# A four-layer graph network on one core: PSUM banks in the schedule, fewer row transposes, weights behind x, the last graph in pieces

## The chip, the core and the metric

The kernel runs on one core of a Trainium2 chip. The core has a matrix engine (TensorE, PE in the profile; PEld is its loading of stationary operands), a vector engine (VectorE, DVE), a scalar engine with activation functions (ScalarE, ACT), a general engine (GpSimd, POOL) and an engine that mainly issues transfers (SyncE, SP). Each works through its own queue in order and waits on semaphores for the others. Matmuls write to PSUM, which has eight banks here, each a tile of 128 x 512 floats; DVE and ACT read the results out. The metric is the time of the whole program on the device in microseconds, of several runs; a profile of one execution stands beside it.

## The reference

There are 32 graphs of 512 nodes with 256 features, x of (32, 512, 256), and adj of (32, 512, 512), integers of 0 and 1. Four layers follow each other, each with its own kind of attention over the graph, on a normalised and rectified input and with a residual:

```python
h = maximum(layernorm(x), 0)
x = x + layer(h, adj, ...)        # four times, layers 0 to 3

# layer 0: att = softmax(((h @ att_W) @ h.T) / 16 + mask); twice: h = tanh(att @ (h @ W + b))
# layer 1: Wh = h @ W.T; e = leaky(src[:, None] + dst[None, :]); softmax over adj > 0; att @ Wh
# layer 2: Hh = h @ W; e = exp(-leaky(s[:, None] + d[None, :])) where adj != 0; elu((e @ Hh) / rowsum)
# layer 3: hW = h @ W; logits = (hW @ a_1).T + hW @ a_2 + (hW @ a_12) @ hW.T
#          att = softmax(leaky(logits) over adj > 0); elu(h @ W_1 + (att @ h) @ W_2)
```

All products are in fp32. The graphs don't depend on each other; within a graph each layer depends on the one before.

## The kernel before

The kernel takes a graph as four tiles of 128 nodes. It doesn't run in a loop at the time of execution: a planner at build time puts all instructions of all 32 graphs in one order, with up to FLIGHT = 5 graphs in progress, so that one graph's matmuls run while another's vector work is done.

Each step of the computation is an `op`: an engine, a cost as a pair (how long it holds its engine, when its result is there), the ops it comes after, a function that emits it, and the tiles it uses. Tiles come from numbered places in pools: 35 pages of SBUF, four value buffers, eight PSUM banks and a few more. `Plan.order` plays the ops through event by event: at each moment every engine takes, of its ready ops, the one with the earliest due time whose places are free. The due time is the graph's number times a distance, less what is still to come after the op; the distance of the last graphs is another one. `Plan.best` tries 32 pairs of distances and keeps the one whose order ends first by the planner's own clock. The ops are then emitted in that order, which fixes the sequence on each engine and each issuing queue; semaphores for the tiles' dependences are added by the framework below, and it, not the plan, decides who waits at run time.

A graph's work runs as follows. x and the adjacency come in by SP's queue (L458, L461); DVE turns the integers into a code, SP's transposing transfers turn it (L478), and masks are made of it. `normed` computes statistics on DVE (L496, L497), a power on POOL (L503), an offset on DVE (L506) and the normalised row on ACT (L510). The result is turned by a transfer on SP (L518) in two 16-bit planes and joined by ACT (L530); the first graph's first layer is turned by PE (L523, out at L526) instead.

Layers 0 and 3 do their block products with seven products in place of eight (`seven`): sums of blocks are formed on DVE (L600), then seven matmuls go alternately into a part p and a part q that accumulate in PSUM, and after each stage a block is copied out by ACT or added to another by DVE before the next product goes into the same place. With `beside` set, p and q are two halves of one bank: bank_f0p and bank_f3p (features, L715, copied out at L723 or L725, added at L730), bank_v0p and bank_w3p (values, L741). Without it, they are two banks: bank_q0p and q0q (L806), bank_s3p and s3q (L983), bank_v3p and v3q (L741).

Layers 1 and 2 need one row of scores spread over all partitions (`leaky_exp_t`). For the first and last five graphs, `turned`, PE makes it by four transposes of a broadcast column (L654, bank_r) and ACT reads it from PSUM (L671). For the others, DVE transposes squares (L658), SP writes the row to DRAM (L662) and reads it back spread over the partitions (L667), and ACT reads it from SBUF.

`attend` (L698, bank_a) multiplies the exponentials with the values for two tiles of nodes at a time, and a column of ones in the values gives the row sums. In layer 0 a second convolution follows (L851, L869). Behind layer 3, `fourth` takes reciprocals (L1063) and adds both terms (L1068), upper3, exp4 and all_terms (L1074, L1078, L1081) make the elu and the residual for two tiles each, and POOL's queue stores the graph in one transfer (L1092).

The weights come in at the start: att_W and W0, which the first graph needs, by ACT's queue (L384), and DVE forms their seven block sums (L361 to L366); the others by POOL's queue (L306), after the first graph's adjacency.

Of the kernel before, what the change touches and what calls it, by code (L numbers as in the profile page):

```python
# [15 lines left out]
AF = mybir.ActivationFunctionType  # L16
# [3 lines left out]
P = 128  # L20
# [8 lines left out]

PE512, PE256, PET = 429.0, 216.0, 112.0
def pe(n512=0, n256=0, nt=0):
    t = n512 * PE512 + n256 * PE256 + nt * PET
    return t, t + 170.0


# [15 lines left out]
class Plan:  # L53
# [3 lines left out]

    PASS = 200.0  # L60


    APART, APART_LAST = [1000.0 * k for k in range(32, 64, 2)], [1000.0 * k for k in (2, 8)]
    LAND, RATE = 2000.0, 200.0
    SLACK = {"V": (1.05, 0.0), "A": (1.05, 0.0), "G": (1.5, 0.0), "D": (1.0, 800.0)}

# [3 lines left out]
    def op(self, engine, cost, after, emit, graph, uses=(), size=0):  # L70


        much, more = self.SLACK.get(engine, (1.0, 0.0))
        cost = cost[0] * much, cost[1] * much + more
        flat = []
        for a in after:
            flat += a if isinstance(a, tuple) else [a]
        o = {"engine": engine, "cost": cost, "after": [a for a in flat if a is not None], "emit": emit,
             "graph": graph, "uses": list(uses), "number": len(self.ops), "size": size, "late": more}
        self.ops.append(o)  # L80
        return o

# [5 lines left out]
    def best(self, pools):  # L88
        for o in self.ops:
            o["depth"] = 0  # L90
        again = True
        while again:
            again = False
            for o in self.ops:
                depth = max((a["depth"] + 1 for a in o["after"]), default=0)
                again |= depth > o["depth"]
                o["depth"] = max(depth, o["depth"])
        apart = min(itertools.product(self.APART, self.APART_LAST), key=lambda a: self.order(pools, *a)[1])
        out, took = self.order(pools, *apart)
        assert len(out) == len(self.ops), "the plan is stuck"  # L100
        return out, took

    def order(self, pools, apart, apart_last):
        free = {pool: list(range(n)) for pool, n in pools.items()}
        users = {}
        for o in self.ops:
            o["left"] = len(o["after"])
            for p in o["uses"]:
                p["users"] = 0
                p.pop("number", None)  # L110
            for a in o["after"]:
                users.setdefault(a["number"], []).append(o)
# [21 lines left out]
        while True:  # L134
            for e in engines:
                skipped = []
                while at[e] <= now and ready[e]:
                    rank, o = heapq.heappop(ready[e])
                    new = [p for p in o["uses"] if "number" not in p]
                    need = [p["pool"] for p in new]  # L140
                    if any(len(free[n]) < need.count(n) for n in need):
                        skipped.append((rank, o))
                        continue
                    for p in new:
                        p["number"] = free[p["pool"]].pop(0)
                    holds, until = o["cost"]
                    if o["size"]:
                        wire = max(wire, now) + o["size"] / self.RATE
                        until = wire - now + self.LAND + o["late"]
                    at[e] = now + holds  # L150
                    out.append(o)
                    heapq.heappush(events, (at[e], next(numbers), None))
                    heapq.heappush(events, (now + until + self.PASS, next(numbers), o))
                for x in skipped:
                    heapq.heappush(ready[e], x)
            if not events:
                break
            now = events[0][0]
            while events and events[0][0] <= now:
                o = heapq.heappop(events)[2]  # L160
                if o is None:
                    continue
                for p in o["uses"]:
                    p["users"] -= 1
                    if not p["users"]:
                        free[p["pool"]].append(p["number"])
                for w in users.get(o["number"], []):
                    w["left"] -= 1
                    if not w["left"]:
                        heapq.heappush(ready[w["engine"]], (w["rank"], w))  # L170
        return out, now if len(out) == len(self.ops) else float("inf")


@with_exitstack
def kernel(
# [35 lines left out]
    HALF = H // 2  # L211
    FLIGHT = 5
    PAGES, VALUES = 35, 4
    LEAD = 2

    const = ctx.enter_context(tc.tile_pool(name="const", bufs=1))
# [81 lines left out]
    def prepare(engine, cost, after, emit, *keys, size=0):  # L298
        return plan.op(engine, cost, after, emit, 0, W.uses(keys), size)
# [80 lines left out]

    ready = {}
    w0_sb, att_sb = raw("raw9"), raw("raw10")
    for n, dst, w, key in (("att", att_s, att_w, "raw10"), ("w0", w0_s, w0, "raw9")):
        ready[key] = [prepare("A", (550.0, 4000.0), [], lambda w=w, key=key: nc.scalar.dma_start(  # L384
            out=raw(key)(), in_=rows_of(w)), key, size=P * HC * H * 4)]
        ready[n] = seven_of(raw(key), dst, HALF, ready[key], key)
    nc.scalar.dma_start(out=b0_sb, in_=line_of(b0))
# [47 lines left out]
    def graph(b, adj_before, x_before):  # L435
# [4 lines left out]
        def op(engine, cost, after, emit, *keys, size=0, weights=()):  # L440
            return plan.op(engine, cost, after, emit, b, T.uses(keys) + W.uses(weights), size)

        def two(g):
            return slice(2 * g, 2 * g + 2)
# [7 lines left out]
        def e(l, c):  # L452

            return T[f"e{l}_{c // 2}"][:, c % 2, :]
# [12 lines left out]
        for t in range(NT):  # L467

            got_adj.append(op("D", D_ADJ, got_adj[-1:] if b else [], partial(fetch_adj, t), "adj", size=P * N * 4))
        if b == 0:  # L470
            for o in loads:
                o["after"] += got_adj[-1:]

# [17 lines left out]
        def normed(l, xs):  # L491
# [41 lines left out]
            done = []  # L533
            for g in range(NT // 2):
                a, d = (op("V", V_STATS, [xs[t]], partial(stats, t), "x", "slot") for t in (2 * g, 2 * g + 1))
                a = op("V", V_TINY, [a, d], partial(variance, g))
                r = op("G", G_POW, [a], partial(root, g))
                r = op("V", V_TINY, [r], partial(offset, g))
# [81 lines left out]
        def scored_values(l, hs, w_aug, ready):  # L620
# [4 lines left out]
            for t in range(NT):  # L625
# [10 lines left out]
                def values(t, key):  # L636
                    nc.scalar.copy(T[f"v{l}"][:, t, LEAD : LEAD + H], T[key][:, :H])  # L637

                a = op("PE", pe(n256=4), [hs[t]] + ready, partial(product, t, key), key, f"hT{l}")
                ss.append(op("V", V_TINY, [a], partial(scores, t, key), key))  # L640
                vs.append(op("A", A_HALF, [a], partial(values, t, key), key, f"v{l}"))
            return vs, ss
# [1 line left out]
        def leaky_exp_t(l, ss, sign):  # L644
# [1 line left out]

            turned = b < FLIGHT or b >= B - FLIGHT
            key = f"bank_r{l}" if turned else f"row{l}"  # L650
            line = []

# [34 lines left out]
        def attend(l, es, vs, use):  # L687


            done, a = [], None  # L690
            lead = LEAD if l < 3 else 0
            for g in range(NT // 2):
                keys = [f"bank_a{l}{2 * g + j}" for j in range(2)]

                def product(g, c, keys):
                    for j in range(2):
                        t = 2 * g + j
                        nc.tensor.matmul(T[keys[j]][:, : LEAD + H + 1 - lead], e(l, c)[:, t * P : (t + 1) * P],  # L698
                                         T[f"v{l}"][:, c, lead:], start=(c == 0), stop=(c == NT - 1))

                for c in range(NT):
                    a = op("PE", pe(n256=4), [es[c], vs[c], a], partial(product, g, c, keys),
                           *keys, f"v{l}", f"e{l}_{c // 2}")
                done += [use(2 * g + j, a, keys[j]) for j in range(2)]
            return done


        def two_tiles(key, start, k):
# [361 lines left out]
            a = op("V", V_TINY, [a], sums, key)  # L1070
            return op("V", V_PSUM, [a, wb[0, t // 2], wb[1, t // 2]], both_terms, key, "y3", "w3")

        def upper3(g):
            nc.vector.scalar_tensor_tensor(T["x"][:, two(g), :], T["y3"][:, two(g), :], -1.0, T["x"][:, two(g), :],  # L1074
                                           ALU.max, ALU.add)

        def exp4(g):
            nc.scalar.activation(T["r3"][:, two(g), :], T["y3"][:, two(g), :], AF.Exp, bias=one)  # L1078

        def all_terms(g):  # L1080
            nc.vector.scalar_tensor_tensor(T["y3"][:, two(g), :], T["r3"][:, two(g), :], 1.0,  # L1081
                                           T["x"][:, two(g), :], ALU.min, ALU.add)

        us = attend(3, es, vs, fourth)
        last = []
        for g in range(NT // 2):
            u = op("V", V_MASK, us[two(g)], partial(upper3, g), "y3", "x")
            l = op("A", A_BIAS, us[two(g)], partial(exp4, g), "y3", "r3")
            last.append(op("V", V_MASK, [l, u], partial(all_terms, g), "y3", "r3", "x"))

        def store():
            nc.gpsimd.dma_start(out=out[b].rearrange("(t p) h -> p t h", p=P), in_=T["y3"])  # L1092

        op("G", G_STORE, last, store, "y3", "slot", "ahead", size=N * H * 4)
        return code, got_x[-1]

    code, got_x = None, [None, None]
# [40 lines left out]
```

## Time and profile before

| | us |
|---|---|
| median of 3 runs | 2413.71 (2413.61 to 2414.37) |
| profiled execution | 2412.91 |
| its span, first to last instruction | 2411.1 |
| PE busy in the span | 2370.4 |
| DVE busy | 2052.5 |
| ACT busy | 1720.6 |
| first matmul begins | 13.46 |
| last run of matmuls begins, and lasts | 2396.03, 7.27 |

The granted clock of PE is 0.999 of full speed. Busy time counts an engine's instructions from start to end; matmuls are pipelined and their ends are modelled, so that they overlap, and the profile's busy PE is not PE at its peak. The time from one matmul's start to the next says more. An instruction of the code that multiplies in fp32 shows in the profile as two matmuls of the same width; a transpose shows as one. Where the profile names a releaser, it is the engine and line whose semaphore came last by the records. Line numbers are those of the kernel before; in the changed kernel the same instructions stand some 32 to 42 lines further down.

### The profile page before, as it was taken

The page shows a single profiled execution, that of the slowest core. Times are in us where ns is not written, and L with a number is a line of the kernel's source. Part 1 is how long each engine was busy: PE and PEld are TensorE (multiplying, and loading weights), DVE is VectorE, ACT ScalarE, POOL GpSimd, SP SyncE. Part 2 cuts the span into 40 slices and gives each one's busy share as a digit, 9 for nine tenths or more (in the row PEclk, how much of TensorE's full clock was granted, in tenths as well). Part 3 has the DMA queues.
Part 4 walks back from the last instruction along what each step waited for, and adds up shares of the span by engine and source line. Part 5 has one row for each costly group of instructions (what it writes and reads, how often), then busy time and mean ns, then how long its engine had stood idle before and what let it go on. Part 6 is the DMA issues. An engine that isn't in the chain of part 4 may idle for free.

```text
span 2411.1 us, 36568 instructions
## 1 busy us (share of the span) xinstructions
PE 2370.4 (98%) x11638; PEld 1983.9 (82%) x11638; DVE 2052.5 (85%) x6316; ACT 1720.6 (71%) x3385; POOL 262.3 (11%) x320
## 2 busy tenths in 40 slices
PE   7999999999999999999999999999999999999998
PEld 5788888888888888888888888888888888887877
DVE  6778889888898888888888988888888898876888
ACT  4567777677777777767777777777777777665885
POOL 3000011101110100101110111101011100110110
PEclk9999999999999999999999999999999999999999
DMA  7311333333323333333323334333333343320221
GB/s 190 90 42 38 73 69 88 74 71 63 86 67 74 86 73 74 82 65 82 84 62 84 72 72 87 70 77 76 67 85 84 62 88 75 84 44 18 49 44 44
DMA packets 429633, 175.55 MB, mean 73 GB/s; under 512 B 385824, under 2 KB 402848, under 8 KB 429440
## 3 DMA queue, kind: packets, MB, share of 16 engines
q1 hardware_dynamic: 423392, 153.81, 30.0%
q0 software_dynamic: 5360, 18.75, 2.5%
q8 instruction: 92, 1.51, 0.3%
q14 instruction: 101, 0.83, 0.1%
q10 hardware_dynamic: 688, 0.66, 0.1%
HBM read 64.49 MB, written 16.87 MB: 34 GB/s over the span
## 4 chain that ended last, share of the span: by engine, by line
PE 90%; issue 3%; ACT 3%; DVE 2%; DMA 2%; SPq 0%; POOL 0%; POOLq 0%; DVEq 0%; ACTq 0%
PE bank_a L698 35%; PE bank_z L851 9%; PE bank_v L630 8%; PE bank_o L869 5%; PE bank_q0p L806 4%; PE bank_s3p L983 4%; PE bank_v0p L741 4%; PE bank_f0p L715 4%; PE bank_w3p L741 4%; PE bank_f3p L715 4%; PE bank_q0q L806 3%; PE bank_s3q L983 3%; PE bank_v3p L741 2%; PE bank_v3q L741 2%; DMA planesT<-planes 1%
## 5 line engine op out<-in xcount | busy, mean ns | idle before, releaser
L698 PE MATMUL bank_a<-v,e 128*128 128x257 f32 (+1 forms) x4096 | 977.3, 381 | 3.2 <-ACT e L1035 1.5
L698 PEld LDWEIGHTS bank_a<-v,e 128*128 128x128 f32 x4096 | 758.0, 190 | 152.4 <-issue 47.9
L503 POOL TENSOR_TENSOR rstd<-ve,mhalf 128x2 f32<-128x2 f32 x256 | 223.0, 884 | 1947.7 <-DVE ve L500 1668.9
L530 ACT COPY hT<-planesT 128x512 uint16<-128x512 uint16 x508 | 380.7, 768 | 70.1 <-DMA planesT<-planes 69.3
L510 ACT ACTIVATE xn<-x,off,rstd 128x256 f32<-128x256 f32 x512 | 277.0, 595 | 45.0 <-DVE off L506 44.6
L630 PE MATMUL bank_v<-l_aug,hT 128*128 128x258 f32 x1024 | 253.6, 381 | 0.5 <-ACT hT L530 0.4
L851 PE MATMUL bank_z<-e,y 128*128 128x512 f32 x512 | 240.7, 592 | 0.7 <-ACT y L842 0.7
L515 DVE COPY planes<-xn 128x512 uint16<-128x512 uint16 x508 | 206.6, 422 | 19.1 <-DMA planesT<-planes 13.7
L630 PEld LDWEIGHTS bank_v<-l_aug,hT 128*128 128x128 f32 x1024 | 190.9, 190 | 28.2 <-ACT hT L530 1.5
L496 DVE BATCH_NORM_STATS2 st<-x 128x6 f32<-128x256 f32 x512 | 210.1, 410 | 0.0
L674 ACT ACTIVATE e<-e 128x512 f32<-128x512 f32 x256 | 151.7, 625 | 0.0
L851 PEld LDWEIGHTS bank_z<-e,y 128*128 128x128 f32 x512 | 95.5, 190 | 68.1 <-issue 56.4
L671 ACT ACTIVATE e<-row,scores 128x512 f32<-128x512 f32 x176 | 118.0, 711 | 13.9 <-DMA row<-row 13.7
L637 ACT COPY v<-bank_v 128x256 f32<-128x256 f32 x256 | 89.2, 376 | 53.8 <-PE bank_v L630 43.9
L869 PE MATMUL bank_o<-w_sb,zT 128*128 128x256 f32 x512 | 120.2, 379 | 0.0
L990 DVE SCALAR_TENSOR_TENSOR e<-bank_s3p,v,mask 128x256 f32<-128x256 f32 x256 | 111.0, 476 | 6.2 <-PE bank_s3p L983 5.1
L497 DVE BATCH_NORM_AGGREGATE mv<-st 128x2 f32<-128x6 f32 x512 | 93.2, 182 | 17.5
L869 PEld LDWEIGHTS bank_o<-w_sb,zT 128*128 128x128 f32 x512 | 96.5, 190 | 13.9 <-DVE st L496 0.2
L725 ACT ACTIVATE fa<-bank_f3p,l_u 128x256 f32<-128x256 f32 x128 | 60.5, 472 | 66.0 <-PE bank_f3p L715 65.6
L814 ACT ACTIVATE e<-e 128x512 f32<-128x512 f32 x93 | 58.6, 630 | 54.6 <-DVE e L823 54.1
L829 DVE TENSOR_TENSOR e<-e,mask 128x512 f32<-128x512 f32 x124 | 85.0, 686 | 9.4 <-ACT e L814 9.3
L892 DVE TENSOR_TENSOR e<-e,mask 128x512 f32<-128x512 f32 x128 | 84.0, 688 | 5.4 <-ACT e L674 5.1
(189 smaller groups left out, 4462.8 us busy)
## 6 DMA issues: line engine op xcount, KB each, us to landing
adj<-in_adj_dram SPq DMA_DIRECT2D x128, 256.0 KB
out_dram<-y POOLq DMA_DIRECT2D x32, 512.0 KB, 4.2
x<-in_x_dram SPq DMA_DIRECT2D x31, 512.0 KB
row<-row SPq DMA_DIRECT2D x44, 256.0 KB
planesT<-planes SPq DMA_TRANSPOSE x508
codeT<-code SPq DMA_TRANSPOSE x128
crest<-crest SPq DMA_TRANSPOSE x64
raw_w<-in_L_gnn_W_dram POOLq DMA_DIRECT2D x3, 256.0 KB, 4.7
```

What stands on the lines that cost most here:

```text
L496: nc.vector.bn_stats(T[f"st{l}"][:, t, :], T["x"][:, t, :])
L503: nc.gpsimd.tensor_tensor(T[f"rstd{l}"][:, two(g)], T[f"ve{l}"][:, two(g)], mhalf[:, two(g)], ALU.pow)
L510: nc.scalar.activation(T[f"xn{l}"][:, t, :], T["x"][:, t, :], AF.Relu, bias=T[f"off{l}"][:, t : t + 1], scale=T[f"rstd{l}"][:, t : t + 1])
L515: nc.vector.tensor_copy(T[f"planes{l}_{t}"], bits)
L530: nc.scalar.copy(bits[:, :, :, t * P : (t + 1) * P], T[f"planesT{l}_{t}"].rearrange("p (b c) n -> p b c n", b=2))
L630: nc.tensor.matmul(T[key][:, :cols], T[f"hT{l}"][:, c, t * P : (t + 1) * P], w_aug[:, c, :], start=(c == 0), stop=(c == HC - 1))
L698: nc.tensor.matmul(T[keys[j]][:, : LEAD + H + 1 - lead], e(l, c)[:, t * P : (t + 1) * P], T[f"v{l}"][:, c, lead:], start=(c == 0), stop=(c ...
L715: nc.tensor.matmul(p[:, : N // 2], w[:, x - 1, :], right(x), start=fresh, stop=True, skip_group_check=True)
L741: nc.tensor.matmul(p[:, j * k : (j + 1) * k], right(x)[:, j * P : (j + 1) * P], w[:, x - 1, :], start=fresh and j == 0, stop=True, skip_gr ...
L806: nc.tensor.matmul(p[:, j * N // 2 : (j + 1) * N // 2], right(x)[:, j * P : (j + 1) * P], left(x), start=fresh and j == 0, stop=True, skip ...
L851: nc.tensor.matmul(T[f"bank_z{k}"], T["y0"][:, c, k * P : (k + 1) * P], e(0, c), start=(c == 0), stop=(c == NT - 1))
L869: nc.tensor.matmul(T[key][:, j * H : (j + 1) * H], T["zT"][:, k, t * P : (t + 1) * P], w1_sb[:, k, :], start=(k == 0), stop=(k == HC - 1))
```

## The change

Four things change. In the planner, `order` no longer lets an op use a PSUM bank while another engine's op in that bank has not ended by the plan's clock, and the pairs of distances are compared by `replay`, which runs a finished order once more with plain costs (without the planner's allowances), with 100 ns for every hand-over between ops, and with the rule that users of a place wait for the former owner and, in a bank, for other engines' users. A price for a matmul of 258 columns is new. Second, PE makes the rows by transposes for the first and last two graphs (TURNED) in place of five. Third, W0 and att_W are issued by SP, behind x of the first graph, their block sums come behind the statistics of the first graph, and the first graph's adjacency comes behind both weights. Fourth, the last graph's last attention is done for tiles 0 and 1 together, then for tile 2, then for tile 3, with the elu by the same parts and a store of each by SP's queue.

```diff
-        apart = min(itertools.product(self.APART, self.APART_LAST), key=lambda a: self.order(pools, *a)[1])
-        out, took = self.order(pools, *apart)
+        apart = min(itertools.product(self.APART, self.APART_LAST), key=lambda a: self.replay(self.order(pools, *a)))
+        out = self.order(pools, *apart)
+        took = self.replay(out)
...
+    def replay(self, order):
...
+        at, end, owners, before, wire = {}, {}, {}, {}, 0.0
+        for o in order:
+            start = max([at.get(o["engine"], 0.0)] + [end[a["number"]] + self.HOP for a in o["after"]])
+            for p in o["uses"]:
+                where = p["pool"], p["number"]
+                owner = owners.get(where)
+                if owner is None or owner[0] is not p:
+                    before[where] = owner[1] if owner else []
+                    owner = owners[where] = p, []
+                waits = before[where]
+                if p["pool"] == "bank":
+                    waits = waits + [x for x in owner[1] if x["engine"] != o["engine"]]
+                start = max([start] + [end[x["number"]] + self.HOP for x in waits])
+                owner[1].append(o)
+            holds, until = o["plain"]
+            if o["size"]:
+                wire = max(wire, start) + o["size"] / self.RATE
+                until = wire - start + self.LAND
+            at[o["engine"]], end[o["number"]] = start + holds, start + until
+        return max(end.values())
...
-                    if any(len(free[n]) < need.count(n) for n in need):
+                    if any(len(free[n]) < need.count(n) for n in need) or any(
+                            t > now for p in o["uses"] if p["pool"] == "bank" for x, t in p["ends"].items() if x != e):
...
+                    for p in o["uses"]:
+                        p["ends"][e] = now + until + self.PASS
...
+    TURNED = 2
...
-    for n, dst, w, key in (("att", att_s, att_w, "raw10"), ("w0", w0_s, w0, "raw9")):
-        ready[key] = [prepare("A", (550.0, 4000.0), [], lambda w=w, key=key: nc.scalar.dma_start(
+    for n, dst, w, key in (("w0", w0_s, w0, "raw9"), ("att", att_s, att_w, "raw10")):
+        ready[key] = [prepare("D", D_X, [], lambda w=w, key=key: nc.sync.dma_start(
...
+            for n in ("raw9", "raw10"):
+                ready[n][0]["after"] += got_x[-1:]
+            for o in got_adj[1:]:
+                o["after"] += ready["raw9"] + ready["raw10"]
...
+                if b == l == 0:
+                    for n in ("w0", "att"):
+                        ready[n][0]["after"].append(d)
...
-            turned = b < FLIGHT or b >= B - FLIGHT
+            turned = b < TURNED or b >= B - TURNED
...
+            return [[0, 1], [2], [3]] if (b, l) == (B - 1, 3) else [[0, 1], [2, 3]]
...
+        def store_part(ts):
+            nc.sync.dma_start(out=out[b].rearrange("(t p) h -> p t h", p=P)[:, ts, :], in_=T["y3"][:, ts, :])
...
+            if b == B - 1:
+                op("D", D_OUT, last[-1:], partial(store_part, ts), "y3", "slot", "ahead", size=N * H)
...
-        op("G", G_STORE, last, store, "y3", "slot", "ahead", size=N * H * 4)
+        if b < B - 1:
+            op("G", G_STORE, last, store, "y3", "slot", "ahead", size=N * H * 4)
```

## The prediction

> **What bounds the kernel now.** I read the page's engine shares first, then the chain of waits, then the groups of TensorE (PE) by shape, the list of waits, and last the timeline at the start, at one stall in the middle and at the end.
>
> The page's engine shares, and the shares of its chain of waits by engine: PE is busy throughout, and the chain is PE nearly throughout.
>
> ```profile
> PE 2370.4 (98%) x11638; PEld 1983.9 (82%) x11638; DVE 2052.5 (85%) x6316; ACT 1720.6 (71%) x3385; POOL 262.3 (11%) x320
> ...
> PE 90%; issue 3%; ACT 3%; DVE 2%; DMA 2%; SPq 0%; POOL 0%; POOLq 0%; DVEq 0%; ACTq 0%
> ```
>
> Two of PE's groups by shape (count, busy us and mean ns, idle before), two of its waits (us, times, longest), and two runs of the chain in order of time (start, length, count): the mean of one matmul is well over what one takes in a run, and the waits of PE that recur are for readers of bank_f0p.
>
> ```profile
> L698 PE MATMUL bank_a<-v,e 128*128 128x257 f32 x3072 | 729.5, 380 | 1.6 <-ACT r L935 0.8 <-DVE e L919 0.6 <-DVE e L892 0.2
> L654 PE MATMUL bank_r<-ident,scores 128*128 128x128 f32 x80 | 21.7, 273 | 0.0
> PE bank_f0p L715 <- ACT fa L723: 8.2, 20, 0.5
> PE bank_f0p L715 <- DVE fa L730: 1.7, 4, 0.4
> 528.39 2.62 PE bank_v L630 x12
> 558.20 13.01 PE bank_a L698 x60
> ```
>
> The timeline (start, length) at the start, at one such stall, and at the end: what the first matmul comes behind, who is in the bank between two matmuls, and what follows the last one.
>
> ```profile
> 6.81 0.29 DVE L361 COPY att_s<-raw_w 128x256 f32<-128x256 f32 x1 [5.93 <-DMA raw_w<-in_L_gnn_att_W_dram]
> 8.09 0.42 DVE L496 BATCH_NORM_STATS2 st<-x 128x6 f32<-128x256 f32 x1
> 13.46 0.97 PE L523 MATMUL bank_n<-ident,xn 128*128 128x128 f32 x3 [13.46 <-ACT xn L510]
> 531.70 0.59 PE L715 MATMUL bank_f0p<-hs,att_s 128*128 128x256 f32 x2
> 532.13 0.61 PE L741 MATMUL bank_v3p<-l_aug,hT 128*128 128x129 f32 x4
> 532.33 0.42 DVE L730 TENSOR_TENSOR fa<-fa,bank_f0p 128x256 f32<-128x256 f32 x1 [0.66 <-PE bank_f0p L715]
> 532.79 0.37 ACT L723 COPY fa<-bank_f0p 128x256 f32<-128x256 f32 x1 [0.85 <-DVE fa L730]
> 533.21 0.70 PE L715 MATMUL bank_f0p<-hs,att_s 128*128 128x256 f32 x2 [0.47 <-ACT fa L723]
> 2396.03 7.27 PE L698 MATMUL bank_a<-v,e 128*128 128x259 f32 x32 [0.17 <-ACT e L1035]
> 2405.11 0.69 DVE L1081 SCALAR_TENSOR_TENSOR y<-r,x 128x512 f32<-128x512 f32 x1
> 2406.10 0.75 POOL L1092 DMA_DIRECT2D out_dram<-y  x1 [4.88 <-DVE y L1081]
> ```
>
> So PE is the bound. Its busy time overlaps itself (a mean of 380 ns, yet 60 in a row in 13.01 us), so I count by pitch, the time from one start to the next in an unbroken run. 257 columns: 13.01/60 = 0.217 us. 258: 2.62/12 = 0.218. 256: 16 in 3.45 = 0.216. 512: 0.429. 128 or 129: 0.111. With the counts by shape: 3072 x 0.217 + 2047 x 0.218 + 3190 x 0.216 + 536 x 0.429 + 2760 x 0.111, and 3 for the narrow ones, is about 2341 us. The span is 2411.1. Of the other 70 us, 13.5 lie before the first matmul, 7.8 behind the last (2403.30 to 2411.1), and about 49 are holes. Those three are all that a reordering can win; only removed matmuls lower the 2341.
>
> **What the Trainium skill says.** "PSUM — Partial Sum Buffer", section on bank collisions, says that two engines must not be in the same bank and quadrant at once, two readers included, and that software must guard by bank. The trace agrees with the consequence: at 532.33 VectorE (DVE) reads bank_f0p, ScalarE (ACT) reads other columns of it only afterwards (532.79, released by DVE), and PE writes it again only after that (533.21). "DMA: Bandwidth & Descriptors", section "Latency and other measured facts", gives about 0.6 us to the first byte for a transfer issued by SP and about 1 us by POOL, and under "Issuing engines are not separate DMA queues" that all issuers share the same 16 DMA engines. For the first, no SP store of output exists in this trace; the second agrees with the start, where x and two weights, issued by two engines within 2 us, all come late.
>
> **The change part by part.**
>
> Row transposes. TURNED 2 in place of FLIGHT 5 takes graphs 2, 3, 4 and 27, 28, 29 off the PE route: 6 graphs x 2 layers x 4 = 48 of the 80 transposes of L654. At a pitch of 0.111 us that is 5.3 us of PE work, and PE is the bound: -5.3. In their place come 12 square transposes on DVE (0.305 each, 3.7 us over the run, beside PE), 24 SP transfers (0.55 and 0.53 to issue), and 48 ACT passes at 711 ns in place of 692. In the middle 44 such trips show no wait of PE for a row, only 13.7 us of ACT in 14 waits. I take 0 for this cost; from above see the last rival.
>
> Bank rule in the plan (order, replay). No instruction changes; the order does. A block in seven goes PE, then one or two readers of its bank, then PE into the same bank. That trip is 0.6 us with one reader (0.16 us of matmul tail, a read of 0.37, two hand-overs) and 533.21 - 532.13 = 1.08 with two. PE needs that much other work in between. From the two orders of instructions I summed PE's own work at its pitch between one matmul of a bank and the next one into it that carries a wait. Before, 94 such places have under 0.9 us of cover (37 in f0p, 21 f3p, 14 v0p, 17 w3p, 5 elsewhere); after, 23. Missing cover against a trip of 0.9 is 19.7 us before and 4.0 after; against 0.7, 10.6 and 2.3; against 1.1, 38.8 and 8.7. The middle fits the trace: PE's waits for readers of these banks add up to 13.7 us in about 36 waits, and 0.16 of tail in each makes 19.5. So -16, with -8 and -30 as ends.
>
> What the new order may add. Pulling blocks apart delays their consumers and uses cover that other waits had: exponentials for L698, normalised rows for L630. The order alone can't show those. Below: 0, since PE has always one of five graphs to work on. Above: 10 us, a third of the roughly 30 us of holes not caused by these banks. I take +3.
>
> Weights behind x. At present the DVE stands at L361 until 6.81 for att_W, and only then comes the first statistic of x; L361 to L366 for W0 (9.17 to 10.4) stand between its second and third. After: W0 and att_W are issued on SP behind x of graphs 0 and 1, both L361 blocks behind all statistics and the first offset. x alone then has the DMA engines after b0: 0.64 MB, which the start moved by about 5 us (bins of 1 us: 0, 37, 102, 146, 251, 366 GB/s, slow at first). Four statistics of 0.6 from about 4.8 end at 7.2, 0.2 for variance, 1.0 for POOL, 0.2 for the offset, 0.65 for ACT: first matmul at 9.3, not 13.46. Then the adjacency, now behind x of graphs 2 and 3 and both weights, is later: 3.7 MB ahead of its end in place of about 2.8, some 14 to 15 us, not 11.92. Four turns (12.73 to 18.02 to issue, mask at 23.03) lead from there to the mask at about 26, and the first L698, now at 31.6, may start at about 27 with the products before it done. SP queues x and adjacency of later graphs behind it, needed much later. Gain -4.2; ends -1 (the mask decides) and -5.5.
>
> Last graph in pieces. The first pair of tiles leaves earlier, the third and fourth tile one by one; PE's 32 matmuls stay 32. After PE's last, today: reciprocal, two L1068 (0.85), exponential 0.72, L1081 0.69, to 2405.80; with one tile 0.43, 0.47 and 0.42, so 0.85 less. The store: packets of 512 KB ran some 1.6 us at 350 GB/s, 128 KB needs 0.4; minus 1.2, and SP rather than POOL perhaps 0.3 more against a further queue entry. -2.2, ends -1 and -3.5. PE258 in place of PE256 only changes the plan's price.
>
> Sum against the profiled execution: -5.3 - 16 + 3 - 4.2 - 2.2 = -24.7, span 2386.4. That execution took 2412.91, 1.8 above its span, and the median is 2413.71, 0.8 above it: 2389.
>
> **Rivals.** (1) The waits move. The banks' holes close, but PE meets others, for exponentials and normalised rows, and the mask takes most of the start's gain: -5.3 - 8 + 5 - 1.5 - 1.5, about -12, 2402. For it: ACT waits already 44.6 us for offsets and 69.3 for turned planes. Against: PE hardly waits for these now.
> (2) More falls than the banks' part: with trips priced at 1.1 and no new waits, -5.3 - 28 - 4 - 2.2 is -39, 2374. For it: 49 us of holes. Against: drain and fill keep some.
> (3) Nothing to measure: replay's order differs but the machine's queues absorb it, and the mask eats the start: -5.3 + 3, 2411.
> (4) Slower: the row's trip is exposed. In the middle it takes from the first L662 at 395.7 to the first L671 at 404.1, 8.4 us, hidden by four other graphs. Graphs 2 to 4 and 27 to 29 run where fewer are in flight and SP is busiest. 12 x 8.4 is 101 us; it outweighs the 25 gained from a quarter exposed. At half: 2389 + 50, about 2439. For it: the second slice from the start and the one at 2280 to 2340 (56.33 us busy of 60) hold larger holes already. Against: no PE wait for a row in 44 trips.
>
> **How the numbers follow.** Forecast 0.60, its own range 2380 to 2398; (1) 0.22; (2) 0.07; (3) 0.05; (4) 0.06. The range 2380 to 2402 holds the forecast's and most of (1), leaving out (2), (3), (4) and the tail of (1), about 2 in 10. A difference within 0.2% (4.8 us) can't be told from none. Faster: 0.60 + 0.22 + 0.07, less a little for (1)'s tail: 0.88. Same 0.06, slower 0.06.
>
> **What would show it.** L654 falls from 80 to 32. PE's waits for L723, L725, L730 fall from about 13 us to under 4. First matmul at about 9.3, first L698 about 27. The span ends within 6 us of PE's last matmul. It would be wrong if PE's first wait names become L671, L1035 or L530 with over 10 us, or if the mask's DMA is what the first L698 waits for.

## The result, and the profile after

The changed kernel takes 2375.67 us (median of 4 runs, 2375.45 to 2376.26), the one before, run beside it, 2413.66 (2412.87 to 2414.37): a ratio of 0.984, 95% interval 0.983 to 0.986. That is 38 us off, where the forecast took off 25. The profiled execution has a span of 2373.7 us.

The engine shares and the chain's shares by engine, on the page of the changed kernel:

```profile
PE 2347.7 (99%) x11590; PEld 1985.6 (84%) x11590; DVE 2056.8 (87%) x6330; ACT 1720.1 (72%) x3386; POOL 251.6 (11%) x319
...
PE 94%; DVE 3%; ACT 2%; DMA 0%; issue 0%; SPq 0%; POOL 0%; DVEq 0%; ACTq 0%
```

PE has 48 matmuls fewer, its share is up and "issue" is down to 0% of the chain. The next fence has PE's group of row transposes by shape and, from its list of waits (us, times, longest), those that touch the steps of the prediction and the two longest new ones:

```profile
L693 PE MATMUL bank_r<-ident,scores 128*128 128x128 f32 x32 | 8.8, 275 | 0.8 <-DVE scores L673 0.8
PE bank_n L559 <- ACT xn L546: 9.1, 1, 9.1
PE bank_a L736 <- DVE e L823: 3.0, 1, 3.0
PE bank_a L736 <- ACT y L884: 2.2, 1, 2.2
PE bank_f3p L757 <- DVE fa L772: 0.6, 1, 0.6
PE bank_f0p L757 <- DVE fa L772: 0.2, 1, 0.2
PE bank_f3p L757 <- ACT fa L767: 0.2, 1, 0.2
```

The readers of bank_f0p and bank_f3p (now L765, L767, L772), for which PE waited 26 times and 10.4 us in the list of the kernel before, are down to three waits and 1.0 us. The first matmul comes at 9.1, not 13.5. New waits are there: the first attention product stands 3.0 us for the masked exponentials of L823, and a later one 2.2 us for ACT's L884.

The busy time of PE, PEld, DVE, ACT and POOL in the stretch from 240 to 2220 us, clear of the first and the last graphs, for the kernel before and for the changed one (the stretch and its length, busy us and count of each engine, the granted clock, the DMA engines' share and GB/s):

```profile
240.00:2220.00 1980.00, 1967.47 (x9665) 1652.16 (x9664) 1704.78 (x5240) 1437.49 (x2825) 211.25 (x239) 1.00 0.34 73
```

```profile
240.00:2220.00 1980.00, 1979.56 (x9789) 1680.30 (x9788) 1736.95 (x5337) 1463.93 (x2882) 205.77 (x243) 1.00 0.33 76
```

In the same 1980 us the changed kernel gets 124 more matmuls done and PE is idle for 0.4 us in place of 12.5. The start, and then the end, in the changed kernel's timeline:

```profile
4.61 0.43 DVE L532 BATCH_NORM_STATS2 st<-x 128x6 f32<-128x256 f32 x1 [3.73 <-DMA x<-in_x_dram]
9.07 2.35 PE L559 MATMUL bank_n<-ident,xn 128*128 128x128 f32 x8 [9.07 <-ACT xn L546]
18.50 0.68 DVE L511 TENSOR_SCALAR code<-adj 128x1024 bf16<-128x1024 int32 x1
20.09 5.15 SPq L514 DMA_TRANSPOSE codeT<-code  x4
31.77 3.34 PE L736 MATMUL bank_a<-v,e 128*128 128x257 f32 x8 [2.98 <-DVE e L823]
```

```profile
2356.50 11.55 PE L736 MATMUL bank_a<-v,e 128*128 128x259 f32 x52
2367.70 3.53 SPq L1125 DMA_DIRECT2D out_dram<-y  x3
2369.18 0.16 DVE L1105 RECIPROCAL rs<-bank_a 128x1 f32<-128x1 f32 x1
2370.44 0.42 DVE L1122 SCALAR_TENSOR_TENSOR y<-r,x 128x256 f32<-128x256 f32 x1
```

x is no longer behind a weight's block sums. The code, though, is computed at 18.5, because DVE is busy with other work until then, and its turn ends so late that the first L736 begins at 31.8, no earlier than before (31.6). Two pieces of the chain of waits in front of this L736 (start, length):

```profile
23.98 5.58 DMA codeT<-code
29.69 1.01 DVE mask L522
```

So the first attention product does wait for the mask, and the mask for its DMA, which the prediction had named as a sign of being wrong. At the end, 52 matmuls run without a hole, and from the start of the last one 6.0 us pass to the end of the span, where it was 8.2. These 6.0 us divide differently from the 8.2: up to the end of DVE's last instruction 3.2 us in place of 2.9, and from there to the end of the span 2.8 in place of 5.3. The first part is no shorter, because DVE is still busy with the tile before when PE has finished the last one; it takes up the last tile, with the reciprocal of L1105, at 2369.18.

To set all kernels side by side I took from each trace the time from one PE start to the next, less the pitch of the first of the two, and call what is left a hole. "Bank" holes are those in front of the block products (f0, f3, v0, v3, w3, q0, s3), "other" the rest:

| us | before | changed | difference |
|---|---|---|---|
| up to the first matmul | 13.46 | 9.07 | -4.4 |
| pitch of all matmuls | 2339.4 | 2334.1 | -5.3 |
| bank holes | 35.4 | 5.9 | -29.5 |
| of these 240 to 2220 us | 27.7 | 0.8 | -26.9 |
| other holes | 14.8 | 18.8 | +4.0 |
| of these before 60 us | 4.0 | 7.6 | +3.6 |
| last start to the end | 8.21 | 6.00 | -2.2 |

With the rounded pitches of the prediction the pitch of all matmuls comes out 2.4 us higher in both kernels and the other holes as much lower; the differences stay the same within 0.1.

### The profile page after: what moved, and what is told of

Read it like the earlier page. It is cut to its first block, busy times and chain, and to the rows that moved or that the text cites. A ratio compares the mean times of both kernels' runs of the same rounds, so it can differ in the third digit from the quotient of the medians.

```text
span 2373.7 us, 36569 instructions
## 1 busy us (share of the span) xinstructions
PE 2347.7 (99%) x11590; PEld 1985.6 (84%) x11590; DVE 2056.8 (87%) x6330; ACT 1720.1 (72%) x3386; POOL 251.6 (11%) x319
## 4 chain that ended last, share of the span: by engine, by line
PE 94%; DVE 3%; ACT 2%; DMA 0%; issue 0%; SPq 0%; POOL 0%; DVEq 0%; ACTq 0%
PE bank_a L736 35%; PE bank_z L893 9%; PE bank_v L669 9%; PE bank_o L911 5%; PE bank_s3p L1025 5%; PE bank_q0p L848 4%; PE bank_f3p L757 4%; PE bank_v0p L783 4%; PE bank_f0p L757 4%; PE bank_w3p L783 4%; PE bank_q0q L848 3%; PE bank_s3q L1025 3%; PE bank_v3p L783 2%; PE bank_v3q L783 2%; ACT e L710 1%; ACT e L713 0%
## 5 line engine op out<-in xcount | busy, mean ns | idle before, releaser
L736 PE MATMUL bank_a<-v,e 128*128 128x257 f32 (+1 forms) x4096 | 979.8, 381 | 6.0 <-DVE e L823 3.0
L736 PEld LDWEIGHTS bank_a<-v,e 128*128 128x128 f32 x4096 | 758.3, 190 | 155.3 <-issue 55.3
L539 POOL TENSOR_TENSOR rstd<-ve,mhalf 128x2 f32<-128x2 f32 x256 | 215.9, 871 | 1875.1 <-DVE ve L536 1584.4
L710 ACT ACTIVATE e<-row,scores 128x512 f32<-128x512 f32 x224 | 150.7, 713 | 16.3 <-DMA row<-row 16.0
L713 ACT ACTIVATE e<-e 128x512 f32<-128x512 f32 x256 | 150.3, 624 | 0.0
L1077 ACT ACTIVATE e<-e 128x512 f32<-128x512 f32 x128 | 78.1, 629 | 22.7 <-DVE e L1074 22.0
L915 DVE SCALAR_TENSOR_TENSOR z<-bank_o,rs,b_sb 128x256 f32<-128x256 f32 x128 | 56.0, 479 | 40.7 <-PE bank_o L911 40.1
L974 ACT ACTIVATE y<-bank_a,rs 128x256 f32<-128x256 f32 x128 | 54.7, 476 | 49.4 <-DVE rs L970 25.9
L1071 ACT ACTIVATE e<-e,zero 128x512 f32<-128x512 f32 x128 | 84.9, 711 | 6.6 <-DVE crest L1049 6.6
```

The source lines that it names most:

```text
L539: nc.gpsimd.tensor_tensor(T[f"rstd{l}"][:, two(g)], T[f"ve{l}"][:, two(g)], mhalf[:, two(g)], ALU.pow)
L736: nc.tensor.matmul(T[key][:, : LEAD + H + 1 - lead], e(l, c)[:, t * P : (t + 1) * P], T[f"v{l}"][:, c, lead:], start=(c == 0), stop=(c == ...
```

## The experiments

The tables give medians; a ratio is to the kernel before, run beside it, with its 95% interval. Holes are of the profiled execution.

**The planner, apart from the rest.** Four kernels: the kernel before with the whole new planner; the changed one with the old; the one before with the bank rule, but compared by the planner's own clock; the one before compared by rerunning, but without the rule.

```diff
# plan_only: class Plan of the changed kernel in the kernel before, and its price of 258 columns
# old_plan: class Plan of the kernel before in the changed kernel
# rule_only: as plan_only, but
-        apart = min(..., key=lambda a: self.replay(self.order(pools, *a)))
+        apart = min(..., key=lambda a: self.order(pools, *a)[1])
# replay_only: as plan_only, but
-                    if any(len(free[n]) < need.count(n) for n in need) or any(
-                            t > now for p in o["uses"] if p["pool"] == "bank" for x, t in p["ends"].items() if x != e):
+                    if any(len(free[n]) < need.count(n) for n in need):
```

> The kernel before with the new planner alone (bank rule, replay, price of 258 columns); transposes, weights and last graph as before. Theory T (the holes are round trips through a PSUM bank that the old plan did not know of, and the new one covers them): most of the gain is here, 25 to 30 us of 38, so about 2384 to 2389, with fewer than 20 PE holes over 60 ns in front of the block products between 240 and 2220 us. Rival R (the other three parts make room on PE and at the ends, and the order matters little): about 2400, with the holes still there.

> The changed kernel with the old planner: transposes, weights and last graph as in the changed one. T: about -5.3 for the transposes, -2 for the end and -1 to -4 for the start, so 2402 to 2406, with about 25 us of holes in front of the block products in the middle. R: below 2392.

> The kernel before with the bank rule in the order, but the pairs of distances still compared by the planner's own clock. T with the rule as its cause: the same as plan_only within 4 us. Rival C (the comparison by rerunning finds the better order): above 2400.

> The kernel before with the comparison by rerunning, but without the bank rule in the order. T: only a better pick among orders that all have the holes, 2403 to 2412. C: within 5 us of plan_only.

| | us | ratio | bank holes 240 to 2220 us (number) | bank holes, all | other holes, all |
|---|---|---|---|---|---|
| plan_only | 2398.21 | 0.994 (0.992 to 0.995) | 5.1 (21) | 14.9 | 21.9 |
| rule_only | 2397.47 | 0.994 (0.992 to 0.995) | 2.9 (13) | 17.0 | 18.7 |
| replay_only | 2418.21 | 1.002 (1.001 to 1.003) | 23.4 (134) | 32.0 | 20.6 |
| old_plan | 2415.32 | 1.001 (1.000 to 1.002) | 30.2 (149) | 36.3 | 30.2 |

The rule is the cause of the missing bank holes, and the comparison by rerunning is not: rule_only and plan_only agree within 1 us, and rerunning without the rule leaves 134 holes and is 4.4 us slower than the kernel before, outside the 2403 to 2412 that T gave. But both of my sums were off. The new planner alone gave 15.6 us, not 25 to 30, because it traded: bank holes fell by 20.5 us, others rose by 7. And the three other parts with the old planner gave nothing that can be told, where adding their first matmul (8.28), their tail (6.18) and their transposes makes -12.5: the old planner dealt them an order with 16 us more of holes. The largest sum in PE's list of waits in old_plan, after the first matmul's, is again in a bank, though another:

```profile
PE bank_v0p L752 <- DVE v L802: 7.6, 24, 0.3
```

So neither theory T nor its rival R holds as written: the parts don't add.

**The trip through the bank, made longer.** The copy of layer 0's features out of PSUM is done twice, in both kernels, each in its own unchanged order. The outcome is the same; ACT's read of the bank lasts 0.35 us longer.

```diff
                         nc.scalar.copy(block(i, l_), T[key][:, : N // 2])
+                        nc.scalar.copy(block(i, l_), T[key][:, : N // 2])
```

> The kernel before with the copy of layer 0's features out of PSUM done twice in a row, the same value both times and the same order of instructions: the trip through bank_f0p is 0.35 us longer at its ACT reads, and ACT has 43 us more to do. T: some 40 places with less than 1.2 us of cover grow by up to 0.35 us each, +8 to +16 us. Rival L (ACT's load, not the trip, makes the holes): the same growth here and in the changed kernel.

> The changed kernel with the same copy done twice, in its own order. T: its cover is mostly over 1.2 us, so +1 to +5 us. L: +8 us or more, like the other one.

Before went to 2431.17, +18.3 us (ratio 1.007, 1.006 to 1.009); the changed kernel to 2383.29, +7.6 over its 2375.67. PE's waits for the copies, in the first (they were 8.2 us in 20) and in the second, with the longest one that names bank_f0p:

```profile
PE bank_f0p L715 <- ACT fa L724: 21.3, 30, 1.0
```

```profile
PE bank_f0p L757 <- DVE fa L773: 0.9, 3, 0.4
```

The same 43 us of ACT work cost the old order 14.6 us of bank holes in the middle (27.7 to 42.3) and the new one 6.0 (0.8 to 6.8). ACT also reads the banks of other block products, so its load alone (L) would have shown there too. It doesn't: 14.4 of the 14.6 us stand in front of the products into bank_f0p, whose copy is doubled (17.6 to 32.0 us), and those of all other banks together change by 0.2. In the changed kernel 4.2 of the 6.0 are in bank_f0p. So the trip is the cause; both amounts are over what T gave, by 2 to 3 us.

**Row transposes.** TURNED at 5, as before, and at 0, in the changed kernel.

```diff
-    TURNED = 2
+    TURNED = 5        # turned5; 0 in turned0
```

> The changed kernel with rows by PE transposes for five graphs at each end again. Theory H (a row by PE also holds one of eight banks until four ACT passes have read it, which the bank rule turns into holes at both ends): 5.3 us of transposes and 5 to 10 us of holes more, mainly between 60 and 420 us and after 1900, so 2386 to 2391. Rival P (transposes cost their pitch alone): 2381.

> The changed kernel with every row through DRAM. P and a hidden trip: 32 transposes of 0.111 us less, 2372. Rival E (the trip of some 8 us is exposed where few graphs are in progress): holes in the first 240 us and after 2220 us grow by more than 3.6 us, 2376 or more.

turned5 took 2380.32 (ratio 0.986, 0.985 to 0.988), 4.7 us over the changed kernel. The number is P's, and in the trace the pitch is 5.3 us more while the holes are the same in sum (0.3 us less), so H falls; the holes do stand elsewhere, 2.7 us fewer between 60 and 420 us and 3.4 more after 1900. turned0 took 2380.51 (0.986, 0.985 to 0.988), although its pitch is 3.6 us less: its holes are 30.0 us in place of 24.7 (in its profiled execution, the fastest of the four with 2377.10). The two largest sums in PE's list of waits in turned0 after that for the first matmul:

```profile
PE bank_a L736 <- DVE e L961: 4.7, 4, 3.6
PE bank_s3p L1025 <- DVE fs L639: 3.1, 1, 3.1
```

Neither names a row. E's time is there, but not its place: before 240 and after 2220 us together the holes are some 3 us fewer than in the changed kernel, and between these some 8 us more. So E isn't shown. A new order of the instructions, as tried further down, moves the time by as much as either of these two edits.

**The start and the end, one at a time.** The changed kernel with the weights as before, with the last graph as before, and with x of graphs 2 and 3 behind graph 0's adjacency.

```diff
# no_weights: the four edits of the weights undone
# no_pieces: parts() gives [[0, 1], [2, 3]] always, and POOL stores every graph
# adj_first
-        got_x = [op("D", D_X, [x_before], partial(fetch_x, ts), "x", "ahead", ...)
+        got_x = [op("D", D_X, [x_before] + (first_adj if b in (2, 3) else []), partial(fetch_x, ts), "x", "ahead", ...)
...
+            first_adj.extend(got_adj[1:])
```

> The changed kernel with W0 and att_W by ACT's queue and their block sums first, as before. Theory A (parts add up): the first matmul 4.4 us later, so 2380. Rival W (the start's order carries on: graphs 1 to 3 are normalised earlier, and the holes between 60 and 240 us shrink with it): 2384 to 2390. Rival D (every edit deals the order of the first and last graphs anew, and their holes vary by some 5 to 10 us either way): anywhere from 2376 to 2390, with the holes of the first and last phases not those of the changed kernel.

> The changed kernel with the last graph's tiles in pairs and one store by POOL, as before. A: the tail from the last matmul 2 us longer, 2378. D: the same plus up to 5 us either way from the holes of the last phase.

> The changed kernel with x of graphs 2 and 3 behind the adjacency of graph 0 on SP's queue, so that the code, its turn and the mask come earlier than x of later graphs. A: the hole of 3 us in front of the first L736 goes, 2372 to 2374. D: that hole goes, but the order of the next graphs is dealt anew, 2370 to 2382.

| | us | first matmul | holes to 60 us | holes 60 to 240 | holes from 2220 | last start to end |
|---|---|---|---|---|---|---|
| changed | 2375.67 | 9.07 | 8.1 | 4.9 | 7.4 | 6.00 |
| no_weights | 2380.69 | 13.37 | 2.4 | 5.2 | 9.0 | 6.33 |
| no_pieces | 2381.76 | 8.46 | 8.4 | 5.0 | 12.7 | 7.82 |
| adj_first | 2377.05 | 8.69 | 4.5 | 10.4 | 6.6 | 6.34 |

no_weights costs 5.0 us. That is about what A gave for its late first matmul, but A's account doesn't fit: its first 60 us have 5.7 us fewer holes, more than the 4.3 us by which it starts later, and what it loses it loses behind, 3.6 us of holes between 240 and 2220 us and 1.6 after that. This is as D had it, and what the weights' place is worth by itself isn't shown. no_pieces costs 6.1, not 2: 1.8 in the tail, and 5.3 us of holes in the last phase, where the last graph's products come together and wait for its exponentials (no_pieces' timeline):

```profile
2363.51 8.95 PE L736 MATMUL bank_a<-v,e 128*128 128x259 f32 x32 [3.30 <-ACT e L1077]
```

The kernel before has the same pairs and only 0.17 us in front of the same 32 matmuls, so pairs alone don't make this hole; it too is D's. In adj_first the hole for the mask is gone, the first attention product begins 3.4 us earlier (adj_first's timeline):

```profile
28.38 1.14 PE L737 MATMUL bank_a<-v,e 128*128 128x257 f32 x4
```

and yet the time is 1.4 us more, for between 180 and 240 us 8.4 us of holes stand in place of 3.5. That is D: the next graphs were dealt anew.

**Nothing changed but the deal.** The planner's allowance for a hand-over, PASS, at 220 in place of 200, in both kernels; it changes no instruction, only the order. And two wider choices for rerunning: 256 pairs of distances, and 64 pairs at four allowances.

```diff
-    PASS = 200.0
+    PASS = 220.0      # pass_220 (changed kernel), before_pass_220 (kernel before)
# wide
-    APART, APART_LAST = [1000.0 * k for k in range(32, 64, 2)], [1000.0 * k for k in (2, 8)]
+    APART, APART_LAST = [1000.0 * k for k in range(32, 64)], [1000.0 * k for k in (1, 2, 3, 4, 6, 8, 10, 12)]
# wide_pass
+    APART, APART_LAST = [1000.0 * k for k in range(32, 64, 2)], [1000.0 * k for k in (1, 2, 4, 8)]
+    PASSES = [150.0, 200.0, 250.0, 300.0]
```

> The changed kernel with the planner's allowance for a hand-over at 220 ns in place of 200: no work changes, only the order is dealt anew. D: 2370 to 2386, with 240 to 2220 us free of bank holes (under 5 us) and the ends different. A: within 1.5 us of the changed kernel.

> The kernel before with the old planner's allowance at 220 ns in place of 200. T: the holes in front of block products between 240 and 2220 us stay between 22 and 32 us; the time is within 8 us of 2413 either way. Rival M (the old order was an unlucky one): the holes in the middle fall by half, below 2400.

> The changed kernel with 256 pairs of distances in place of 32 to choose from by rerunning. If rerunning ranks orders as the chip does: 2368 to 2374. If it can't tell them apart at this size: 2376 to 2383.

> The changed kernel with 64 pairs of distances at four allowances, 150 to 300 ns, to choose from by rerunning. As for the wider choice of distances: 2366 to 2374 if rerunning ranks orders, 2376 to 2383 if not.

pass_220 took 2382.38 (0.987, 0.986 to 0.989), 6.7 us more, with 2.9 us of bank holes in the middle: the ends differ, the middle hardly, as D had it. before_pass_220 took 2405.86 (0.997, 0.996 to 0.998), 7.4 us less, and its bank holes in the middle are 65 with 11.5 us, not 123 with 27.7. T's time, within 8 us of 2413, came out, but its 22 to 32 us is refuted: a good part of what the rule removes depends on the order that the old planner happened to deal. M is right on the holes, not on the time: other holes in the middle rose from 5.0 to 11.5. The same stretch of the middle in before_pass_220:

```profile
240.00:2220.00 1980.00, 1972.34 (x9705) 1658.61 (x9704) 1707.39 (x5271) 1432.84 (x2838) 201.92 (x241) 1.00 0.32 73
```

wide took 2377.12 (2375.73 to 2381.38) and wide_pass 2376.24 (2372.12 to 2378.55): neither can be told from the changed kernel. More orders to choose from bought nothing that these runs can show, and no median here is below the changed kernel's.

Over all kernels, bank holes between 240 and 2220 us are 11.5, 23.4, 27.7 and 30.2 us in the four without the bank rule, and at most 7.0 in the eleven with it, leaving aside the two with the doubled copy (42.3 and 6.8). The amount depends on the deal: between the two kernels with the allowance at 220 they fall by 8.6 us, not by 26.9, and the whole change is worth 23.5 us, not 38.

## Why the prediction was wrong

What failed is the size of one term: "So -16, with -8 and -30 as ends" for the bank rule. The bank holes fell by 29.5 us, at the far end of what I had written down. With -29.5 in the place of -16 the sum is -38.

The other terms add up to what was measured, but only in part for the reasons that I gave. The transposes took 5.3 us of pitch, as worked out. The tail's -2.2 is right by luck: the work behind the last matmul, which I had 0.85 us shorter, is 0.3 us longer, and the store, which I had some 1.3 us sooner, ends 2.5 us sooner after DVE's last instruction. Of the start's -4.2, the first matmul did come 4.4 us sooner, but the holes before 60 us grew by 3.6. These make up nearly all of the +4.0 of other holes, which looks like my +3 for what the new order may add; in the middle, where that cost should have been, other holes fell by 1.6 us. So -4.2 and +3 are each off, and only their sum came out near (-1.2 worked out, -0.4 measured).

The price of the bank rule was wrong for two reasons that the trace of before had in it.

First, I priced all trips at 0.9 us, between 0.6 for one reader and 1.08 for two, and took this because it met PE's listed waits. I have since gone through the 123 bank holes over 0.06 us in the middle of the kernel before. The dearest kind is the one shown in the prediction: 16 trips through bank_f0p with DVE and then ACT, each of 1.08 us, 8.4 us of holes in all. It is one place of the order, which comes back with nearly every graph. With ACT alone, five trips took 0.63 us. The number of readers isn't all, though: four trips with DVE alone took 1.04 to 1.11 us, and four with ACT alone 3.5, because the reader came late. Here (start, length) DVE is at the scores of L634 before it reads the bank; the trip through the same bank that follows, with ACT alone, is a short one:

```profile
825.99 0.35 DVE L634 COPY scores<-bank_v 128x2 f32<-128x2 f32 x4
826.26 0.41 DVE L730 TENSOR_TENSOR fa<-fa,bank_f0p 128x256 f32<-128x256 f32 x1
826.73 0.70 PE L715 MATMUL bank_f0p<-hs,att_s 128*128 128x256 f32 x2 [0.45 <-DVE fa L730]
827.26 0.61 PE L741 MATMUL bank_v3p<-l_aug,hT 128*128 128x129 f32 x4
827.46 0.37 ACT L723 COPY fa<-bank_f0p 128x256 f32<-128x256 f32 x1 [1.61 <-PE bank_f0p L715]
```

Counted at 1.1, the prediction has 38.8 and 8.7 us of missing cover before and after; the holes were 35.4 and 5.9. It is no law. Counted at 1.1 from the traces, wherever a reader stands between two matmuls of a bank, old_plan has 32 us (at 0.9 only 7) for 36.3 us of holes and before_pass_220 25 for 17.7, but replay_only 56 for 32.0, plan_only 8 for 14.9 and rule_only 8 for 17.0.

Second, a wait's idle time in the list is less than what it costs. Of the 123 holes, 61 are of 0.10 us in the matmul that directly follows the one that waited, the second of the pair that an fp32 product makes: 6.3 us that no list of waits puts down to the bank. Only the time from start to start shows it. Over the whole run this kind fell from 8.2 to 1.3 us, and all other bank holes from 26.4 to 4.2. So of the 13.5 us that I missed, about 7 are a term that I had put at nothing, and about 6 are the price of the trips, 22 us where I had 16. I had the start-to-start total (about 49 us of holes) and still split it by the list, 19.5 for the banks and "roughly 30 us of holes not caused by these banks". By start to start it was 35.4 and 14.8.

The mechanism was right: the rule fills the trip with other work (rule_only, replay_only), the holes are the trip's (before_twice, bank by bank), and PE's waits for the readers of the features fell below the 4 us that I had named. "PSUM — Partial Sum Buffer" in the Trainium skill, in its section on bank collisions, asks for a guard by bank; the runs show what it costs when the plan doesn't count on it.

The steps for the start were half right. The first matmul came as worked out, but the first attention product was to begin at about 27 and began at 31.8. I had reckoned with the adjacency landing late; it was DVE's place for the code, behind planes of the next graph, at 18.5, that was late, and the mask's DMA behind it. Rival (1), the waits move, was true of the new planner on its own (+7 of other holes in plan_only); of the changed kernel one half of it is true, that the mask takes most of the start's gain. Rival (2), priced at 1.1, came to 2374 and was nearest in number; its chance of 0.07 was too low, since it rested on the same count as the forecast with one price changed. Its account is only half right: other holes did grow, and part of what fell is the second matmul. Rival (3) had the mask right, but not the rest. Rival (4) is refuted for TURNED = 2 by the time; in PE's list no wait names a row, and the two for exponentials of L710, which ACT makes from rows, are of 1.1 and 0.5 us.

What the prediction didn't have at all is that a plan's parts don't add. Its steps were each counted against the order before, and by those terms the new planner alone should have been worth 13 (measured 15.6) and the other three parts 12 (measured none: +1.5, which can't be told from nothing). An edit that changes no work moved one kernel by +6.7 and the other by -7.4. So some of the 38 us is luck: the order before was the slower of the two that ran, and the one after the fastest of four. How much can't be settled here: with the rule and all four parts, four deals took 2375.67, 2382.38, 2377.12 and 2376.24. The two kernels with the allowance at 220 are 23.5 us apart, close to the 24.7 of my sum, but that doesn't bear the sum out, since I had counted on the other two orders.

## What to carry to other kernels

Where PE is the bound, measure its holes from start to start less the pitch, and put them down by the tile of the matmul that comes late; a list of waits leaves out the tail and the slower second matmul. Price the round trip through a PSUM bank by the readers that follow each other in it and by when each comes to it, at the most common costly kind, and let the planner know of it. And where a scheduler deals the order, test a part by its effect beside an edit that changes no work: here differences under some 8 us were within what a new deal does, and in the changed kernel no part but the planner moved the time by more.

## What the runs showed of the hardware

A matmul right behind one that waited starts 0.10 us later than its pitch: in the kernel before, 78 of the 89 holes over 0.12 us are followed by one of 0.10 or 0.11 us. The prediction's lines show it too, where the pair at 533.21, behind a wait, lasts 0.70 us and the pair at 531.70 lasts 0.59. So a wait of PE mostly costs that in addition. A bank with two readers, DVE and then ACT, is free for PE again after 1.08 us, the same in all 16 trips, against 0.63 for ACT's read alone where it comes at once. ACT's read begins only behind DVE's although they read different columns; the trace names DVE's semaphore as what released it, so this is the order that the program asks for, and no run here shows what would happen without it.
